# Summing a scan's pairs over the states by accumulating transfers within SBUF instead of by TensorE with the identity

## The chip, the cores and the metric

The kernel runs on one core of a Trainium2 chip. The metric is the device time of one execution in microseconds; the time before is the median of three runs. The engines are called as in the profile: PE (TensorE, with PEld for its weight loads), DVE (VectorE), ACT (ScalarE), POOL (GpSimd) and SP (SyncE, which issues most transfers).

## The reference, cut to what matters

Layer 0 is a convolution block with a Mamba scan, layer 1 attention and a mixture of eight experts. The change lies in the scan. For every batch image, in four chunks of 32 channels, it computes over a sequence of 4096 positions and N = 16 states:

```
delta = softplus(dt @ dt_proj_w.T + dt_proj_b)
dA  = exp(delta[..., None] * A)
dBu = delta[..., None] * Bm[:, :, None, :] * xin[..., None]

def step(h, inp):
    dA_t, dBu_t, C_t = inp
    h = dA_t * h + dBu_t
    y = jnp.einsum('bdn,bn->bd', h, C_t)      # the sum over the 16 states
    return (h, y)

y = y + D_skip * xin
out = y * silu(z) @ out_proj_w.T
```

The change concerns how the sum over n in y is formed. Everything is float32.

## The kernel before, in words

**Blocks, halves, states.** The sequence of one image is cut into 8 blocks of 512 positions, and there are 4 images, so 32 blocks. A block has two halves p (two channel chunks each, which fill 128 partitions), and each half has the 16 states n. A unit is one (image, block, half, state): 1024 units in all. The main loop walks through them, one unit to a slot.

**A slot.** SP fetches the B and C rows of a later unit (`rows`, three slots ahead, four buffers). ACT makes `da` two slots ahead. DVE runs three instructions on 128x512 tiles in `scan`: h = rows*du, the scan itself, and hc = rows*h, the term of this state for y. Into the same slot go one group of attention work (four score matmuls `sc`, two exponentials `pT`, and four `av` matmuls of the group before) and some stages of two lanes, X and Y. These are lists of generators for all other work: normalisations, convolution and projections of the next blocks in lane Y, the end of a block (`closed`) and the end of the network (`finished`) in lane X. Attention starts only when the first blocks of an image are closed, and a stretch of attention is left over after the last unit.

**Order.** Each engine's instructions are chained in the order in which the program writes them (`queued`), so an engine that waits for one instruction holds back all that is written after it. Waits between engines come from the tiles that instructions share, and from buffers of a pool that are taken again.

**The sum over the states.** In the first 128 slots (`ALONE`, half an image, where there is little attention yet) each term hc goes to PE one slot later and is added into one PSUM tile y by a matmul with the identity: 16 matmuls to a sum. After that POOL adds the odd state's term to the even one's (`gpsimd.tensor_add(even, even, hc)`), and PE adds the pair's sum into y two slots later: 8 matmuls to a sum. Each such matmul of float32 is two records in the trace. After the last one `scanned` lets DVE compute xin = xin*dsk + y and POOL multiply it by the gate zs; when the second half of a block is done, `closed` is put at the head of lane X.

**Buffers.** The terms hc have five buffers before. PSUM tile y has one.

A profile shows nearly all instructions under line 445, that of the recording helper, so groups are told apart by their tiles.

Of the kernel before, what the change touches and what calls it, by code (L numbers as in the profile page):

```python
# [9 lines left out]
F32 = mybir.dt.float32  # L10
# [3 lines left out]
ALU = mybir.AluOpType  # L14
# [3 lines left out]
P = 128  # L18
C = 128
EPS = 1e-5  # L20
BLK = 512
# [3 lines left out]
NST = 16  # L25
# [11 lines left out]
def conv_mamba_attn_moe_kernel(ctx: ExitStack, tc: tile.TileContext, t: dict):  # L37
    nc = tc.nc
    x, out = t["x"], t["out"]
# [19 lines left out]
    ident = const.tile([P, P], F32, name="ident")  # L59
# [379 lines left out]
    class Queue:  # L439
# [7 lines left out]
    tensor, vector, scalar, gpsimd, sync = (  # L447
        Queue(e) for e in (nc.tensor, nc.vector, nc.scalar, nc.gpsimd, nc.sync)
    )

    def mm(out, lhsT, rhs, start=True, stop=True):
        tensor.matmul(out, lhsT=lhsT, rhs=rhs, start=start, stop=stop)
# [11 lines left out]
    def flush():  # L464
        for entry in outgoing:
            entry[0] -= 1
            if entry[0] == 0:
                sync.dma_start(out=entry[1], in_=entry[2])
        outgoing[:] = [entry for entry in outgoing if entry[0]]
# [7 lines left out]
    def pool(name, bufs=1, space=None):  # L477
        return main.enter_context(
            tc.tile_pool(name=name, bufs=bufs, **({} if space is None else {"space": space}))
        )  # L480

    mix, att, side = pool("mix"), pool("att"), pool("side")
# [249 lines left out]
    def fetched(b, i, p, n):  # L732

        bcd = in_of[b, i, p][4]
        w = mix.tile([P, 2, BLK], F32, name="rows", bufs=4)
        sync.dma_start(
            out=w.rearrange("p k q -> p (k q)"),
            in_=bcd[:, n, :][None].to_broadcast([DI, 2, 2 * BLK]),
        )
        return w  # L740

    def decayed(b, i, p, n):
        da = mix.tile([P, BLK], F32, name="da", bufs=3)
        scalar.activation(da, in_of[b, i, p][2], AF.Exp, scale=amat[:, n : n + 1])
        return da

    def scan(b, i, p, n, w, da):

        du = in_of[b, i, p][3]
        h = mix.tile([P, BLK], F32, name="h", bufs=3)  # L750
        vector.tensor_mul(h, w[:, 0, :], du)
        vector.tensor_tensor_scan(
            out=h, data0=da, data1=h, initial=0.0 if i == 0 else states[b % 2][:, p, n : n + 1],
            op0=ALU.mult, op1=ALU.add,
        )
        hc = mix.tile([P, BLK], F32, name="hc", bufs=5)
        vector.tensor_mul(hc, w[:, 1, :], h)
        return h, hc

    def scanned(b, i, p, y):  # L760
        xin, zs, delta, du, bcd = in_of.pop((b, i, p))
        vector.scalar_tensor_tensor(xin, xin, dsk, y, ALU.mult, ALU.add)
        gpsimd.tensor_mul(zs, xin, zs)
        gated[b, i, p] = zs
# [185 lines left out]
    def weighted(group):  # L950
        b, q, h, pTs, first, last, prev, final = group
        if first:
            sums[0] = ps_av.tile([P, BLK], F32, name="av")
        av = sums[0]
        for k, (v, pT) in enumerate(pTs):
            for u in range(2):
                mm(
                    av[64 * u : 64 * u + 2 * DH, :], v, pT[:, u, :],
                    first and k == 0, last and k == STEP - 1,
                )  # L960
        if last:
            avs = att.tile([P, BLK], F32, name="avs", bufs=2)
            scalar.copy(avs, av)
            if prev is not None:
                gpsimd.tensor_add(avs, avs, prev)


            if not final:
                partial[b, q, h] = dram.tile([P, BLK], F32, name=f"avd{q}{h}")
                send(partial[b, q, h], avs, 3)  # L970
                return
            if h == 0:
                total[b, q] = dram.tile([2, 2, NH, DH, BLK], F32, name=f"total{q}")
            d = total[b, q]
            send(d[:, :, h].rearrange("u k r q -> (u k) r q"), avs, 3)
            if h == NH - 1:
                work_left = inverted(b, q)
                later.extend((slot + n, work_left) for n in (4, 6, 8))
# [148 lines left out]
    def advance(lane, second):  # L1127

        if inside[lane] != second:
            return False  # L1130
        while True:
            if lane not in running:

                tasks = lanes[lane] if lanes[lane] or slot < len(units) else lanes["X"]
                if not tasks or not all(k in done for k in tasks[0][2]):
                    return False
                key, stages, _ = tasks.popleft()
                running[lane] = key, stages(lane) if callable(stages) else stages
            key, stages = running[lane]
            try:  # L1140
                next(stages)
                inside[lane] = not second
                return True
            except StopIteration:
                assert not second
                done.add(key)
                del running[lane]

    def until(key):
        while key not in done:  # L1150
            flush()
            count = len(done)
            moved = [
                advance(*half) for half in (("X", True), ("Y", False), ("Y", True), ("X", False))
            ]
            assert any(moved) or len(done) > count, key
# [17 lines left out]
    for k in range(-2, len(blocks)):  # L1174
        if 0 <= k:
            b, i = blocks[k]
            Y.append((("in", b, i, 1), inputs(b, i, 1), [("scan", *blocks[k - 1], 1)] if k else []))
        if k + 2 < len(blocks):
            b, i = blocks[k + 2]
            if k + 2 == 0 or i > 0:  # L1180
                upper(k + 2)
        if 0 <= k + 1 < len(blocks):
            b, i = blocks[k + 1]
# [20 lines left out]
    ALONE = NB // 2 * 2 * NST  # L1204
    rows, decays, old, due = {}, {}, None, deque()
    even, y_of, waiting, slot = None, {}, None, 0
    while slot < len(units) or due or waiting or left or later or lanes["X"] or running:
        flush()

        for ahead in range(slot if slot == 0 else slot + 3, min(slot + 4, len(units))):  # L1210
            until(("in", *units[ahead][:3]))
            rows[ahead] = fetched(*units[ahead])
        if old:
            (b, i, p, n), h = old
            if i < NB - 1:
                scalar.copy(states[b % 2][:, p, n : n + 1], h[:, BLK - 1 : BLK])
            old = None
        for ahead in range(slot if slot == 0 else slot + 2, min(slot + 3, len(units))):
            decays[ahead] = decayed(*units[ahead])
        group = next(groups, None)  # L1220
        if slot < len(units):
            unit = units[slot]
            h, hc = scan(*unit, rows.pop(slot), decays.pop(slot))
            old = unit, h
            b, i, p, n = unit

            if slot < ALONE:
                due.append((slot + 1, unit, hc, n == 0))
            elif n % 2 == 0:
                even = hc  # L1230
            else:
                gpsimd.tensor_add(even, even, hc)
                due.append((slot + 2, unit, even, n == 1))
        advance("X", True)
        advance("Y", False)
        while due and due[0][0] <= slot:
            _, unit, term, first = due.popleft()
            b, i, p, n = unit
            if first:
                y_of[b, i, p] = ps_y.tile([P, BLK], F32, name="y")  # L1240
            mm(y_of[b, i, p], ident, term, first, n == NST - 1)
            if n == NST - 1:
                scanned(b, i, p, y_of.pop((b, i, p)))
                done.add(("scan", b, i, p))
                if p == 1:
                    lanes["X"].appendleft((("closed", b, i), closed(b, i), []))
        advance("Y", True)
        if waiting:
            weighted(waiting)
        waiting = group  # L1250
        advance("X", False)
        while later and later[0][0] <= slot:
            next(later.popleft()[1])
        slot += 1
# [6 lines left out]
    with tc.If(nc.values_load(general[0:1, 0:1]) > 0):  # L1261
# [4 lines left out]
        with tc.For_i(0, B, 1) as b:  # L1266
# [3 lines left out]
                out=t_tok.rearrange("p k c -> p (k c)"),  # L1270
                in_=tsave[bass.ds(b, 1)].rearrange("o p q -> (o p) q"),
# [96 lines left out]
```

## The time and the profile before

| | |
|---|---|
| time before | 5587.63 us, median of 3 (5581.73 to 5599.81) |
| profiled execution | span 5600.4 us, mean granted PE clock 0.944 |
| POOL adds of pairs, hc<-hc | 448, 655.8 us busy, 1465 ns mean |
| PE matmuls y<-hc,ident | 1152 records, 661.5 us busy |
| DVE scans h with a start state | 896, 1311.3 us busy, 1464 ns mean |
| DVE products hc<-rows,h | 1024, 802.2 us busy, 783 ns mean |
| DVE xin<-xin,w_dsk,y | 64, 47.6 us busy; 91.5 us idle before them |
| data moved | 1097.91 MB, mean 196 GB/s |
| hardware queue q1 | 1093.17 MB, 58.5% of 16 engines' span |

Busy time is the time in which an engine had at least one instruction of the group running. Slices cut the span into 40 equal parts of 140 us, and a digit is the busy share in tenths. The chain of work that ended last is followed back from the last instruction: shares there say which work stood on the path that set the end. A line of waits names the waiting engine and tile, what it waited for, and then the total in us, how often, and the longest. In a group's line the idle time after the second bar is that of the engine just before these instructions.

### The profile page before, as it was taken

How to read it: one execution, taken by the hardware profiler on the slowest of the kernel's cores; microseconds unless marked ns; L12 is line 12 of the kernel's file. 1: busy time of each engine (PE TensorE's matmuls, PEld its weight loads, DVE VectorE, ACT ScalarE, POOL GpSimd, SP SyncE). 2: the span in 40 equal slices, each digit the busy share in tenths (PEclk: the TensorE clock that was granted, in tenths of full speed). 3: DMA queues.
4: the chain of work that ended last, by engine and by line, in shares of the span. 5: the costliest groups of instructions: out<-in, count | busy, mean ns of one | idle time of the engine just before them, and what ended most of it. 6: DMA issues, size and time to landing. Idle time of an engine off the chain costs nothing.

```text
span 5600.4 us, 60586 instructions
## 1 busy us (share of the span) xinstructions
PE 4916.5 (88%) x17866; PEld 2040.8 (36%) x17866; DVE 4174.5 (75%) x6275; ACT 3892.2 (69%) x5957; POOL 2161.8 (39%) x1885
## 2 busy tenths in 40 slices
PE   4666798988999988999998899898999989899997
PEld 2222333333333333333333333333333333344343
DVE  4888877887888888887887888887888888741221
ACT  3455587787777777787777777687777777666553
POOL 2333444454444444445443444444444443320000
PEclk7777799999999999999999999999999999999998
DMA  3455566666666666667665556666765666654432
GB/s 95 169 171 176 194 210 210 205 228 211 230 208 203 210 208 216 205 225 229 224 211 192 192 200 213 219 221 209 232 223 202 206 205 209 210 183 154 147 121 67
DMA packets 427635, 1097.91 MB, mean 196 GB/s; under 512 B 48401, under 2 KB 131746, under 8 KB 427298
## 3 DMA queue, kind: packets, MB, share of 16 engines
q1 hardware_dynamic: 426130, 1093.17, 58.5%
q8 instruction: 144, 2.36, 0.2%
q14 instruction: 193, 1.58, 0.1%
q10 hardware_dynamic: 1168, 0.80, 0.1%
HBM read 941.95 MB, written 135.00 MB: 192 GB/s over the span
## 4 chain that ended last, share of the span: by engine, by line
PE 45%; DVE 21%; ACT 15%; issue 7%; POOL 6%; DMA 5%; SPq 1%; DVEq 0%; ACTq 0%; POOLq 0%
PE av L445 17%; DVE h L445 11%; PE sc L445 10%; PE ps_X L445 8%; PE ps_Y L445 5%; ACT pT L445 5%; PE y L445 4%; ACT L445 3%; ACT xt L445 3%; DVE hc L445 2%; DVE cm L445 2%; POOL rsY L445 1%; POOL rsX L445 1%; DMA ks<-kd 1%; ACT da L445 1%
## 5 line engine op out<-in xcount | busy, mean ns | idle before, releaser
L445 ACT ACTIVATE pT<-sc 128x1024 f32<-128x1024 f32 x2048 | 1983.7, 1022 | 1017.6 <-PE sc L445 1015.2
L445 PE MATMUL av<-pT,v 128*64 128x512 f32 x8192 | 2004.9, 610 | 3.5 <-ACT avs L445 3.3
L445 DVE TENSOR_TENSOR_SCAN h<-da,state,h 128x512 f32<-128x512 f32 x896 | 1311.3, 1464 | 118.6 <-ACT da L445 26.8
L445 PE MATMUL sc<-qs,ks 128*128 128x512 f32 x4096 | 1308.8, 440 | 96.9 <-DMA ks<-kd 51.9
L445 POOL TENSOR_TENSOR hc<-hc 128x512 f32<-128x512 f32 x448 | 655.8, 1465 | 1718.7 <-DVE hc L445 1513.3
L445 PEld LDWEIGHTS sc<-qs,ks 128*128 128x128 f32 x4096 | 717.7, 193 | 773.7 <-ACT pT L445 283.0
L445 PEld LDWEIGHTS av<-pT,v 128*64 128x64 f32 x8192 | 501.6, 137 | 1193.3 <-issue 1105.8
L445 DVE TENSOR_TENSOR h<-rows,du 128x512 f32<-128x512 f32 x1024 | 830.6, 811 | 88.0 <-ACT state L445 38.1
L445 DVE TENSOR_TENSOR hc<-rows,h 128x512 f32<-128x512 f32 x1024 | 802.2, 783 | 78.3 <-DVE h L445 2.3
L445 ACT ACTIVATE da<-delta,amat 128x512 f32<-128x512 f32 x1024 | 749.4, 732 | 9.4 <-DVE h L445 5.2
L445 PE MATMUL y<-hc,ident 128*128 128x512 f32 x1152 | 661.5, 662 | 62.4 <-DVE hc L445 51.3
L445 ACT ACT_TABLE_LOAD x319 | 409.3, 1283 | 22.9 <-PE ps_Y L445 17.8
L445 ACT COPY state<-h 128x1 f32<-128x1 f32 x896 | 175.7, 196 | 194.8 <-DVE h L445 194.3
L445 PEld LDWEIGHTS y<-hc,ident 128*128 128x128 f32 x1152 | 219.6, 209 | 213.8 <-DVE hc L445 101.4
L445 POOL TENSOR_SCALAR rsY<-mvY 128x4 f32<-128x4 f32 x99 | 57.5, 581 | 527.3 <-DVE mvY L445 523.2
L445 POOL TENSOR_TENSOR avs<-avs,prev 128x512 f32<-128x512 f32 x64 | 89.3, 1396 | 438.1 <-ACT avs L445 319.7
L445 PE MATMUL ps_X<-share,w_ew 128*128 128x512 f32 x448 | 223.9, 622 | 20.5 <-DVE share L445 20.2
L445 ACT ACTIVATE xt<-ps_Y,shiftY,rsY 128x128 f32<-128x128 f32 x380 | 143.2, 462 | 129.9 <-POOL shiftY L445 122.4
L445 POOL TENSOR_SCALAR du<-e 128x512 f32<-128x512 f32 x64 | 145.9, 2280 | 217.2 <-ACT e L445 217.2
L445 DVE TENSOR_TENSOR share<-share,xf 128x1024 f32<-128x1024 f32 x128 | 182.8, 1428 | 51.1 <-DMA share<-sharesY 31.0
L445 DVE RECIPROCAL den<-den 128x32 f32<-128x32 f32 x16 | 5.5, 346 | 265.6 <-DMA den<-total 265.6
L445 DVE TENSOR_TENSOR_SCAN h<-da,h 128x512 f32<-128x512 f32 x128 | 182.9, 1429 | 17.3 <-ACT da L445 4.4
(234 smaller groups left out, 4729.6 us busy)
## 6 DMA issues: line engine op xcount, KB each, us to landing
rows<-bcd SPq DMA_DIRECT2D x1024, 512.0 KB
ks<-kd SPq DMA_DIRECT2D x256, 512.0 KB
qs<-qd SPq DMA_DIRECT2D x129, 512.0 KB
v<-vd SPq DMA_DIRECT2D x256, 256.0 KB
share<-sharesX SPq DMA_DIRECT2D x112, 512.0 KB
pairs<-xn SPq DMA_DIRECT2D x128, 128.5 KB
qd<-hi SPq DMA_DIRECT2D x32, 512.0 KB
qd<-lo SPq DMA_DIRECT2D x32, 512.0 KB
```

The source lines that it names most:

```text
L445: return lambda *args, **kw: queued(op(*args, **kw))
```

## The change

Outside the first 128 slots PE no longer adds the pairs' sums. The pair of states 0 and 1 is summed by POOL into a tile of its own, ysum, in SBUF (two buffers). Each of the seven later pairs is summed by POOL as before, and then a transfer issued from POOL adds it into ysum, reading and writing SBUF (`accum_op=ALU.add`). PE's 448 identity matmuls of these slots fall away; those of the first 128 slots stay. `scanned` still comes two slots after the last state and reads ysum. The terms hc have four buffers in place of five. What it is for: TensorE is the engine with the largest busy share, and this sum needs none of its multiplying.

```diff
-        hc = mix.tile([P, BLK], F32, name="hc", bufs=5)
+        if n == 0 and slot >= ALONE:
+            hc = mix.tile([P, BLK], F32, name="ysum", bufs=2)
+        else:
+            hc = mix.tile([P, BLK], F32, name="hc", bufs=4)
         vector.tensor_mul(hc, w[:, 1, :], h)
         return h, hc
...
             if slot < ALONE:
                 due.append((slot + 1, unit, hc, n == 0))
             elif n % 2 == 0:
                 even = hc
             else:
                 gpsimd.tensor_add(even, even, hc)
-                due.append((slot + 2, unit, even, n == 1))
+                if n == 1:
+                    y_of[b, i, p] = even
+                else:
+                    gpsimd.dma_start(out=y_of[b, i, p], in_=even, accum_op=ALU.add)
+                if n == NST - 1:
+                    due.append((slot + 2, unit, None, False))
...
             if first:
                 y_of[b, i, p] = ps_y.tile([P, BLK], F32, name="y")
-            mm(y_of[b, i, p], ident, term, first, n == NST - 1)
+            if term is not None:
+                mm(y_of[b, i, p], ident, term, first, n == NST - 1)
             if n == NST - 1:
                 scanned(b, i, p, y_of.pop((b, i, p)))
```

## The prediction

> **What bounds the kernel now.** I read four views in this order: the page's busy shares and slices (is any engine full, and where), busy time by stretch, the chain that ended last (what a unit of saved work is worth), and the waits of VectorE (who holds whom). First the page, sections 1 and 2.
>
> ```profile
> PE 4916.5 (88%) x17866; PEld 2040.8 (36%) x17866; DVE 4174.5 (75%) x6275; ACT 3892.2 (69%) x5957; POOL 2161.8 (39%) x1885
> ...
> PE   4666798988999988999998899898999989899997
> ...
> DVE  4888877887888888887887888887888888741221
> ...
> DMA  3455566666666666667665556666765666654432
> ```
>
> Between the fifth and the thirty-fifth slice PE is near full, DVE stands at 8 and DMA at 6. After that there are no more scan slots, only attention. The change touches slots 128 to 1023; the following stretch runs from slot 156 to the last scan.
>
> ```profile
> 700.00:4966.00 4266.00, 3885.40 (x14502) 1612.82 (x14502) 3519.72 (x5126) 3210.24 (x4922) 1873.88 (x1582) 0.97 0.63 213
> ```
>
> The columns are PE, PEld, DVE, ACT, POOL, then granted clock, DMA share and GB/s. The stretch holds 868 scans (counted in the timeline of DVE), so a slot takes 4266/868 = 4.91 us: PE is busy for 4.48 of it (91%), DVE 4.05, ACT 3.70, POOL 2.16. PE is the fullest engine, but three of them lie within 0.8 us, and none is at 100%. So a saving on PE can't come through in full: DVE is the next wall at 4.05.
>
> The chain by line (section 4) says what is on the path:
>
> ```profile
> PE 45%; DVE 21%; ACT 15%; issue 7%; POOL 6%; DMA 5%; SPq 1%; DVEq 0%; ACTq 0%; POOLq 0%
> PE av L445 17%; DVE h L445 11%; PE sc L445 10%; PE ps_X L445 8%; PE ps_Y L445 5%; ACT pT L445 5%; PE y L445 4%; ACT L445 3%; ACT xt L445 3%; DVE hc L445 2%; DVE cm L445 2%; POOL rsY L445 1%; POOL rsX L445 1%; DMA ks<-kd 1%; ACT da L445 1%
> ```
>
> The matmuls to remove (y) hold 4% of it, 224 us. DMA holds 5% already, so landings count in this kernel. The waits of DVE from 1000 to 5000 us, longest first:
>
> ```profile
> DVE res L445 <- PE ps_X L445: 69.0, 34, 7.4
> DVE hi L445 <- PE ps_X L445: 68.7, 15, 8.8
> DVE xin L445 <- PE y L445: 65.4, 34, 9.3
> DVE prX L445 <- PE ps_X L445: 50.1, 16, 9.0
> DVE gn L445 <- DMA gn<-in_x: 30.5, 8, 14.1
> DVE aT L445 <- DMA inv<-inverse: 29.0, 12, 6.1
> ```
>
> DVE's waits for PE add up to about 350 us over all rows of that answer; those for DMA to about 100.
>
> [...] The trace of before has no transfer of that kind: all its data went by hardware queues issued from SyncE and ScalarE. [...] The nearest thing in the trace, the pairs<-xn copies within SBUF (four of 128.5 KB), shows 2.37 us at best in the chain of waits and 9.24 us at worst. [...] in one stretch around 4004 us with POOL running without a gap, scans took 2.11 us, where 1.23 to 1.28 us is usual. The POOL adds stay, so this cost stays.
>
> **The change, part by part.**
>
> *Removed from PE.* Outside the first 128 slots there were 448 pair sums of two matmul records each. From 1000 to 5000 us:
>
> ```profile
> L445 PE MATMUL y<-hc,ident 128*128 128x512 f32 x804 | 433.6, 622 | 7.5 <-POOL hc L445 7.5
> ```
>
> 804 records are 402 sums, 1.08 us each, 0.54 us a slot. PE falls to 4.48 - 0.54 = 3.94 us a slot, just under DVE. How much of 0.54 arrives? The chain gives 224 us over the span, 0.25 a slot, as what was surely on the path. DVE's waits for PE, 350 us in 4000, give 0.43 a slot if all vanished. I take 0.30 a slot, 868 x 0.30 = 260 us. The weight loads of y (PEld) lie beside other matmuls and bring nothing more.
>
> *Added: the transfers.* There are 56 sums over 16 states left (64 less 8 in the first 128 slots), with 8 pairs each; the first pair stays where POOL added it, and seven are accumulated, so 392 transfers of 256 KB. The hardware queue moved 1093.17 MB in 58.5% of 16 engines' span: 1093.17/(0.585 x 5600.4) = 334 GB/s while busy. A copy of 256 KB is 0.785 us on all engines[...]. [...] what is in flight beside an accumulation comes later. Some 36 DMA pieces stand on the chain between 700 and 5000 us, mostly 4 to 9 us long; each meets about one accumulation (one per pair of slots, 9.8 us)[...]: 50 us.
>
> *Added: their latency.* In the order of the built program three things wait for it. POOL's next accumulation waits for the one before (336 times). On DVE the multiply writing hc waits for the transfer that reads that buffer, since hc has four buffers now (335 times, three slots after the pair's second term). And xin in scanned, also on DVE, waits for the last transfer (56 times, two slots after the last term), where it waited for PE before. Behind POOL's wait are queued rs and shift of the two lanes, for which ScalarE's xt waits; behind DVE's waits stands the whole scan. The latency L is not in the trace. Lower bound 3.2 us (2.37 us of pairs[...]), upper bound 9.24 us (pairs in a busy stretch). Slot lengths in the stretch: a tenth are at 2.7 us, the quartiles 3.4, 4.5 and 5.8. I stepped through these 868 lengths, each 0.38 shorter but not under 2.72 (which takes the 260 us off), with 1.46 us for POOL's add (its row)[...] and the three waits. The waits then add 10 us for L = 4, 93 for 6, 195 for 7, 349 for 8, 576 for 9. I take L = 6, the middle of the bounds: the transfers have a queue of their own but share engines that are 63% busy. 93 us.
>
> *Added: POOL's time.* [...] Hidden: POOL waited 1386 us for DVE's hc in 4000 us, with nothing else to do.
>
> *Moved.* y lies in SBUF now, so xin reads two SBUF operands (0.75 us as before), and the first hc of a sum comes from its own two buffers, with 16 slots until reuse: nothing. PE's queue loses waits for hc (7.5 us): nothing.
>
> Sum: -260 + 93 + 50 = -117 us, so 5587.6 - 117 = about 5470.
>
> **The rivals.** *(R1) The transfers are hidden wholly.* L at 4 or less, no collisions; PE gives 0.40 a slot: -347 + 10, 5250 us. For: DMA is idle 37% of the time, hc has slack of three slots. Against: gn, inv and pairs already wait for landings. *(R2) The chain of accumulations becomes the bound.* L of 9 to 10 us: the pair can't be shorter than the latency plus its issue, about 10 us against a median of 9.5 for two slots now. Waits of 576 to 866 us, with -260 and +50 as above: 5950 to 6240 us; the sum turns positive already at L of about 7.1. For: 9.24 us on pairs; against: that row queued behind half a dozen transfers of its own ring. *(R3) PE was not the pace-setter.* DVE and the lanes take back the gain, and collisions cost the rest: 5580 to 5600 us. For: PE idles 9% in the stretch; against: 750 us of ScalarE's waits there are pT waiting for PE's sc.
>
> **How the numbers follow.** Forecast 0.45, R1 0.14, R2 with all L above 7.2 0.34, R3 0.07. Faster 0.59, same 0.07, slower 0.34. The time is that of the forecast, 5470. The range runs from R1 (5240) to L of about 8.6 (waits of 475 us, 5850), and leaves out the worse part of R2, some 0.16, and a little under R1.
>
> **What would show it.** Right: y gone from the chain; a slot of 4.6 to 4.8 us; PE down by about 480 us in busy time; a new DVE wait of hc and xin for ysum's transfers below 120 us together; DMA share at 75 to 80%. Wrong: hc or xin waiting for a transfer at the top of DVE's list, or POOL's accumulations waiting for each other for many hundred us (R2); PE idle grown by as much as y gave, with DVE's waits on others instead (R3); DMA share grown by 30 points or more[...].

## The result, and the profile after

The changed kernel takes 5726.09 us (median of four, 5721.36 to 5730.98), the kernel before 5589.66 us beside it: ratio 1.0243, 95% interval 1.0223 to 1.0264, so 136 us slower. The forecast was 5470.

First the page of the changed kernel: the busy shares, and the slices of PE, DVE, the granted clock and DMA.

```profile
PE 4690.0 (82%) x16970; PEld 1936.1 (34%) x16970; DVE 4202.8 (73%) x6275; ACT 3892.2 (68%) x5957; POOL 2480.9 (43%) x2277
...
PE   4676788887888887888888888787888888889997
...
DVE  4888877777888888877887888787887888750221
...
PEclk8777798898999998998999999898998999999998
DMA  3455777777777777777776677777876777764432
```

PE lost 226 us of busy time, although the removed matmuls held 485 (661.5 less the 176.6 of the first 128 slots that stay). The nines of PE turned into eights, and so did some of the clock's: from 700 us on, the granted clock is 0.92 (to 4966 us), where it was 0.97. The columns of the stretch are the same as in the prediction's; the kernel is slower now, so the same stretch holds fewer of its instructions.

```profile
700.00:4966.00 4266.00, 3564.21 (x13229) 1471.71 (x13228) 3446.38 (x5008) 3124.84 (x4813) 2128.81 (x1919) 0.92 0.74 229
```

The last product of a scan starts at 5084.5 us in place of 4966.2 (the tile hc), and what follows is as long as before, 635 us. Slot 128, the first changed one, starts its scan at 575.7 us in place of 576.9. So all the loss lies in the 896 slots that were changed.

The chain that ended last, by engine and by line:

```profile
PE 30%; DVE 19%; POOL 14%; ACT 12%; DMA 12%; issue 10%; SPq 1%; DVEq 0%; POOLq 0%; ACTq 0%
PE av L445 11%; DVE h L445 10%; PE sc L445 7%; PE ps_X L445 6%; DMA ysum<-hc 6%; PE ps_Y L445 5%; ACT pT L445 4%; ACT L445 2%; POOL hc L445 2%; POOL rsY L445 2%; ACT xt L445 2%; POOL rsX L445 2%; POOL du L445 2%; DVE hc L445 2%; DMA ks<-kd 1%
```

PE's share fell from 45% to 30%, and POOL (6% to 14%) and DMA (5% to 12%) took it over. y has left the list, and the transfer stands there with 6%. Tile ysum shows the issue and, last, the time from issue to landing:

```profile
L445 POOL DMA_DIRECT2D ysum<-hc x392: 867/885/1102, 592.2 to 5092.2; - x196
...
DMA to landing us min/median/max: 3.3/5.6/10.5
```

The median landing, 5.6 us, is close to the 6 us that the prediction took, so the surprise isn't in the latency by itself. An issue held POOL for 0.885 us (median).

### The profile page after: what moved, and what is told of

It is laid out like the page before. It is cut to its first block, busy times and chain, and to the rows that moved or that the text cites. A ratio compares the mean times of both kernels' runs of the same rounds, so it can differ in the third digit from the quotient of the medians.

```text
span 5719.6 us, 59540 instructions
## 1 busy us (share of the span) xinstructions
PE 4690.0 (82%) x16970; PEld 1936.1 (34%) x16970; DVE 4202.8 (73%) x6275; ACT 3892.2 (68%) x5957; POOL 2480.9 (43%) x2277
## 3 DMA queue, kind: packets, MB, share of 16 engines
q0 software_dynamic: 56448, 102.79, 10.2%
## 4 chain that ended last, share of the span: by engine, by line
PE 30%; DVE 19%; POOL 14%; ACT 12%; DMA 12%; issue 10%; SPq 1%; DVEq 0%; POOLq 0%; ACTq 0%
PE av L445 11%; DVE h L445 10%; PE sc L445 7%; PE ps_X L445 6%; DMA ysum<-hc 6%; PE ps_Y L445 5%; ACT pT L445 4%; ACT L445 2%; POOL hc L445 2%; POOL rsY L445 2%; ACT xt L445 2%; POOL rsX L445 2%; POOL du L445 2%; DVE hc L445 2%; DMA ks<-kd 1%
## 5 line engine op out<-in xcount | busy, mean ns | idle before, releaser
L445 PE MATMUL av<-pT,v 128*64 128x512 f32 x8192 | 2094.3, 634 | 8.4 <-ACT avs L445 8.1
L445 PE MATMUL sc<-qs,ks 128*128 128x512 f32 x4096 | 1346.0, 450 | 147.2 <-DMA ks<-kd 75.0
L445 POOL TENSOR_TENSOR hc<-hc 128x512 f32<-128x512 f32 x392 | 583.6, 1489 | 1299.6 <-DVE hc L445 1280.6
L445 PEld LDWEIGHTS sc<-qs,ks 128*128 128x128 f32 x4096 | 736.7, 199 | 858.8 <-ACT pT L445 380.7
L445 PEld LDWEIGHTS av<-pT,v 128*64 128x64 f32 x8192 | 518.4, 142 | 1066.7 <-issue 1017.9
L445 DVE TENSOR_TENSOR hc<-rows,h 128x512 f32<-128x512 f32 x968 | 764.7, 790 | 72.9 <-DVE h L445 3.2
L445 POOL DMA_DIRECT2D ysum<-hc x392 | 351.6, 897 | 290.0 <-DMA ysum<-hc 171.7
L445 PE MATMUL ps_X<-ident,xt 128*128 128x128 f32 x372 | 109.4, 365 | 227.4 <-ACT xt L445 218.1
L445 PE MATMUL y<-hc,ident 128*128 128x512 f32 x256 | 176.6, 794 | 52.0 <-DVE hc L445 51.8
```

What stands on the lines that cost most here:

```text
L445: return lambda *args, **kw: queued(op(*args, **kw))
```

## The experiments

Each kernel was timed beside the kernel before on one chip. Since the kernel before read 5589 to 5595 us from one group to the next, differences below are to it within the group. Three theories stood at the start. **C**: without the y matmuls PE pauses long enough to lose its clock, and the relief is eaten. **Q**: POOL's queue. **D**: the load on the DMA engines and late landings.

**The relief alone** (ratio 0.9857, 0.9841 to 0.9874; -80 us).

```diff
-                    gpsimd.dma_start(out=y_of[b, i, p], in_=even, accum_op=ALU.add)
+                    pass
```

> The changed kernel without its transfers: each sum over the states keeps only the pair of states 0 and 1, the other seven pairs are left out. TensorE, VectorE and POOL adds are as in the changed kernel. Theory Q (POOL's queue: the issue, the wait for the transfer before and the wait for its own add hold back rs and shift of the lanes) and theory D (later landings of all transfers): the relief of PE comes through, 5300 to 5400 us, granted clock in the stretch from 700 us on at 0.95 or more. Theory C (without the y matmuls PE pauses long enough for its clock to be cut, 0.97 to 0.92, which eats the relief by itself): 5520 to 5600 us at a clock of about 0.92.

Measured: 5514.27 us. Neither theory has it. Theory C's range begins 6 us above it, and the clock, 0.95 in the stretch, is the one that Q and D expected. The removal of 448 sums is worth 80 us and no more, so the transfers cost 136 + 80 = 216 us on top of it. The stretch, the busy shares and the chain of this run:

```profile
700.00:4966.00 4266.00, 3678.18 (x13956) 1517.65 (x13954) 3571.80 (x5149) 3258.93 (x4981) 1906.60 (x1597) 0.95 0.65 215
...
PE 4614.9 (84%) x16970; PEld 1905.8 (35%) x16970; DVE 4218.7 (77%) x6275; ACT 3889.0 (71%) x5957; POOL 2182.7 (40%) x1885
...
PE 34%; DVE 27%; ACT 16%; DMA 7%; POOL 7%; issue 7%; SPq 1%; DVEq 0%; ACTq 0%; POOLq 0%
```

Two things took the rest. Matmuls overlap on PE, so the 661.5 us of y can't simply be taken off PE's 4916.5. Counted from the trace's records without y's matmuls, PE is busy for 4376.2 us before and for 4456.9 here. So y filled 540.2 us alone before and fills 158.0 here: 382 us of PE's time were freed. Of these, 81 went back because the other matmuls got slower, and 214 because PE's pauses grew, from 684.0 to 897.5 us in all; the traced run is 88 us shorter.

The slowing fits the clock. The trace grants PE either the full clock or half of it; PE worked at half clock for 435.3 us before and for 587.5 here. An estimate of what that costs is half of the difference, 76 us. The pauses are waits for other engines and for landings: DVE rose from 21% of the chain to 27%. DVE's own waits for PE, 1000 to 5000 us, add up to 357.5 us before and 280.5 here, so 77 us of them went.

The fewer hc buffers of the change are in this run too, and cost nothing that shows: the only waits of the product hc are 1.8 us for DVE's own h from 700 to 4900 us, and in the changed kernel it waited 1.4 us for a transfer.

**PE kept busy.** The same matmul on constants, with nothing to wait for and no reader, where each pair's sum stood.

```diff
-                if n == NST - 1:
-                    due.append((slot + 2, unit, None, False))
+                due.append((slot + 2, unit, None, False))
...
+            else:
+                mm(ps_y.tile([P, BLK], F32, name="y"), ident, ew[:, 0:4, :])
```

> The changed kernel, with a matmul on constants (identity and expert weights, result unused) on PE where each y matmul of a pair stood, so PE has the work of the kernel before and no wait for hc. Theory C: the clock returns to 0.95 or more and the time is at or below that of the changed kernel, 5640 to 5730 us. Theories Q and D: the work comes on top, 5800 to 5950 us.

Measured: 5768.65 us (1.0311, 1.0294 to 1.0328), 38 us above the changed kernel for 489 us of work on PE. Its groups on PE, and the one to compare from the changed kernel below:

```profile
L445 PE MATMUL av<-pT,v 128*64 128x512 f32 x8192 | 2005.4, 611 | 3.5 <-ACT avs L445 3.3
...
L445 PE MATMUL y<-w_ew,ident 128*128 128x512 f32 x896 | 488.9, 629 | 0.1
```

```profile
L445 PE MATMUL av<-pT,v 128*64 128x512 f32 x8192 | 2094.3, 634 | 8.4 <-ACT avs L445 8.1
```

Work that nothing waits for took the av matmuls from 634 back to 611 ns. PE's other work, counted as above, is busy for 4532.3 us in the changed kernel and for 4402.3 here, 130 less, and PE's time at half clock fell from 759.6 to 503.2 us; half of that difference is 128. So the clock follows PE's load. The constants and y together fill 543.4 us alone here, where y filled 157.7: about a third of these 386 us came back by the clock. None of the theories has the time: it is 39 us above C's range, and 31 below that of Q and D, which took work on PE at its full length.

The changed kernel's trace shows when. Every stretch at one clock from 700 to 5000 us is 3.41 us or a multiple of it. In the 3.41 us before each of the 111 drops there, PE was busy for up to 62%, a quarter in the median, and in only 16 for less than 1%. Before each return it was busy for at least 83%. Four stretches of 3.4 us, columns as before; the clock is the third number from the end:

```profile
3253.00:3256.40 3.40, 1.20 (x3) 0.29 (x2) 3.16 (x7) 2.93 (x6) 1.49 (x2) 0.98 0.94 287
3256.40:3259.80 3.40, 0.66 (x2) 0.60 (x3) 3.02 (x14) 0.55 (x1) 0.00 (x0) 0.50 1.01 308
3259.80:3263.20 3.40, 3.40 (x7) 1.04 (x6) 2.39 (x3) 2.02 (x3) 1.39 (x2) 0.52 0.90 307
3263.20:3266.60 3.40, 3.40 (x16) 1.63 (x18) 2.10 (x3) 2.86 (x4) 1.70 (x2) 1.00 0.76 169
```

The clock fell at 3256.25 us, 2 us after PE had stopped, in a wait of 4.93 us for a landing of keys. The timeline shows what follows, four score matmuls at the lower clock and, once it had returned, four at the full one:

```profile
3259.14 2.04 PE L445 MATMUL sc<-qs,ks 128*128 128x512 f32 x4 [4.93 <-DMA ks<-kd]
...
3264.34 1.17 PE L445 MATMUL sc<-qs,ks 128*128 128x512 f32 x4
```

**Is DVE the next wall?** For odd states after the first 128 slots the product rows*du is left out, once on the relief alone and once on the kernel before.

```diff
-        vector.tensor_mul(h, w[:, 0, :], du)
+        skip_it = slot >= ALONE and n % 2 == 1
+        if not skip_it:
+            vector.tensor_mul(h, w[:, 0, :], du)
...
-            out=h, data0=da, data1=h,
+            out=h, data0=da, data1=w[:, 0, :] if skip_it else h,
```

> The relief alone, and for odd states outside the first 128 slots the product rows*du is left out (the scan reads rows directly), 448 DVE instructions of about 0.7 us less. Its fall against 5514 us is compared with that of the next run against the kernel before. Theory W (after the relief DVE is the wall): the fall here is larger, 200 to 300 us. Theory C (the clock takes the relief back, whatever DVE does): the falls are alike, within 40 us.

> The kernel before with the same product left out for odd states. Theory W: PE holds it, so it falls by 50 to 130 us only. Theory C: by as much as the run with the relief.

Measured: 5409.61 us (0.9684) on the relief, 99 us below the relief alone; 5533.59 us (0.9903) on the kernel before, 56 us below that. DVE lost 377 us of busy time in the first and 372 in the second, so its work is worth nearly twice as much once y is gone. That is W's direction, but far below its 200 to 300 us, and the falls differ by 44 us, which the noise doesn't tell from the 40 that C allowed: DVE is a larger part of the limit than before, not the wall by itself. How the missing 180 of the 260 us divide between clock and DVE isn't settled, since no run holds the clock.

**Small transfers.** As many issues with as many rows, 16 columns each.

```diff
-                    gpsimd.dma_start(out=y_of[b, i, p], in_=even, accum_op=ALU.add)
+                    gpsimd.dma_start(out=y_of[b, i, p][:, 0:16], in_=even[:, 0:16], accum_op=ALU.add)
```

> The changed kernel with the same 392 accumulating transfers, of 16 columns in place of 512 (the other columns of seven pairs are left out of the sums). POOL issues as many with as many rows; the DMA engines have next to nothing to move. The relief alone gave 5514 us, the changed kernel 5726: 212 us are the transfers. Theory Q (POOL's issue, its wait for its own add and the order of its queue): 5640 to 5700 us. Theory D (the load on the DMA engines and landings that come later): 5520 to 5570 us. The wait for the transfer before and that of xin shrink with the latency, which takes about 32 us (two-sums run) in either case.

Measured: 5640.11 us (1.0092, 1.0074 to 1.0109), +48 us to the kernel before and so 128 us above the relief. It is Q's range, at its lower edge. With hardly any bytes, six tenths of the transfers' cost are there. What POOL waited for at the issue, 700 to 4900 us, and what ScalarE then waited for:

```profile
POOL ysum L445 <- POOL hc L445: 101.4, 331, 1.0
ACT xt L445 <- POOL shiftY L445: 98.5, 64, 4.2
ACT xt L445 <- POOL shiftX L445: 93.3, 40, 7.5
...
POOL ysum L445 <- DMA ysum<-hc: 49.5, 26, 5.5
```

The first line is the issue waiting for POOL's own add, 0.3 us each time. The two lines of xt are the lanes' normalisations behind it in POOL's queue: 192 us together. In the relief alone they read:

```profile
ACT xt L445 <- POOL shiftY L445: 65.1, 53, 2.5
ACT xt L445 <- POOL shiftX L445: 49.2, 37, 4.1
```

PE waits for xt in turn, in the same stretch for 153 us in the relief alone and for 220 here, and pauses.

**POOL's time alone.** A memset without waits where the issue stood, from the second image on.

```diff
-                    gpsimd.dma_start(out=y_of[b, i, p], in_=even, accum_op=ALU.add)
+                    if b:
+                        gpsimd.memset(taps[:, 0:8, :], 0.0)
```

> The relief alone, and in place of each transfer from the second image on (336 of 392) a memset of 128x1024 into the tile of the taps on POOL, about as long as the issue of a transfer, with no wait and no reader; seven pairs of each sum are left out. If POOL's time itself is what the issues cost: 5600 to 5640 us, near the 5640 of the small transfers. If it is the waits of the issue (for POOL's own add, 101 us, and for the transfer before, 50 us): 5520 to 5560 us.

Measured: 5567.14 us (0.9941, 0.992 to 0.9962), 52 us above the relief. A memset took 952 ns, so for 392 issues of 897 ns about 57 us are POOL's time itself, on an engine that is busy for 40% of the span. That is a little above the 5520 to 5560 that was expected if the waits count, and well below the other range. The two xt lines read 90.4 and 64.1 here, so they rise with the time. The other 70 of the 128 go with the issue's waits and the latency of even a small transfer (4.2 us to landing), which weren't taken apart.

**The load without POOL.** Two plain copies of 256 KB for each pair, in the hardware queue, from the second image on.

```diff
-                    gpsimd.dma_start(out=y_of[b, i, p], in_=even, accum_op=ALU.add)
+                    for k in (0, 4) if b else ():
+                        send(taps[:, k : k + 4, :].rearrange("p k c -> p (k c)"), even)
```

> The relief alone, and for each pair from the second image on two plain copies of 256 KB within SBUF, issued by SyncE one slot later into the tile of the taps, which nothing reads; seven pairs of each sum are left out. POOL issues nothing. [...] Theory D: 5650 to 5750 us. Theory Q: 5520 to 5560 us. The copies stand in the hardware queue ahead of rows, so a time above 5750 would be that order and not the load.

Measured: 5562.02 us (0.9952, 0.9941 to 0.9963), 50 us above the relief for 48 of 56 sums, so some 58 for all. That is 2 us above Q's range and 88 below D's: the load is real but small. The DMA share from 700 to 4900 us is 0.75 here and 0.74 in the changed kernel, so the engines are as full. Still it's a figure from a neighbour: copies in another queue aren't accumulations.

**Two sums.** Every other accumulation goes elsewhere, so a transfer waits for the one two pairs back.

```diff
-                    gpsimd.dma_start(out=y_of[b, i, p], in_=even, accum_op=ALU.add)
+                    total_of = y_of[b, i, p] if b == 0 or n % 4 == 3 else taps[:, 0:4, :].rearrange("p k c -> p (k c)")
+                    gpsimd.dma_start(out=total_of, in_=even, accum_op=ALU.add)
```

> The changed kernel, but from the second image on every other accumulation goes into a second tile (that of the convolution's taps, no longer read then), so that a transfer waits only for the one two pairs earlier; the second partial sum is left out of the result. Theory Q: POOL's 247 us of waiting for the transfer before go nearly to nothing and the time falls by 60 to 120 us, to 5600 to 5670. Theories D and C: within 30 us of the changed kernel.

Measured: 5694.45 us (1.0186, 1.0169 to 1.0203), 37 us below the changed kernel, each taken to the kernel before beside it. That is the chain between transfers, as far as this run loosens it: under the 60 to 120 us of Q, and a little over the 30 of D and C. The three parts, 128, 58 and 37, come to 223 against 216. But they aren't separate: the small transfers still wait for one another (49.5 us above), so a piece of the chain is in the 128 as well. That the sum is near doesn't show that the division is right.

**Issue at the slot's end.**

```diff
-                    gpsimd.dma_start(out=y_of[b, i, p], in_=even, accum_op=ALU.add)
+                    late.append((y_of[b, i, p], even))
...
         advance("X", False)
+        for total_of, pair in late:
+            gpsimd.dma_start(out=total_of, in_=pair, accum_op=ALU.add)
+        late.clear()
```

> The changed kernel with each accumulating transfer issued at the end of its slot, after the stages of both lanes, so that rs and shift of that slot stand ahead of it in POOL's queue; same transfers, same waits for one another. POOL alone cost 126 us (small transfers against the relief alone). Theory Q1 (what hurts is that lane work stands behind the issue in POOL's queue): 5620 to 5680 us, and xt waiting for shift falls from 206 us towards the 114 of the relief alone. Theory Q2 (POOL's added time hurts wherever it stands): 5700 to 5740 us.

Measured: 5758.59 us (1.0305, 1.0287 to 1.0322), 33 us above the changed kernel. Q1's mechanism shows and its time doesn't: xt's waits for shift, 700 to 4900 us, fell from 206 to 148 us. But the transfers land later in their slots, and the two lines below were 154.3 and 61.5 us in the changed kernel. So what POOL's order alone costs isn't shown by this run.

```profile
POOL ysum L445 <- DMA ysum<-hc: 284.4, 96, 8.3
...
DVE xin L445 <- DMA ysum<-hc: 187.1, 44, 10.3
```

**Transfers beside the y matmuls.** Both at once, xin reading y in PSUM.

```diff
                 gpsimd.tensor_add(even, even, hc)
+                if n == 1:
+                    ysum = even
+                else:
+                    gpsimd.dma_start(out=ysum, in_=even, accum_op=ALU.add)
```

> PE adds the pairs into y as in the kernel before and xin reads that; beside it POOL issues the 392 accumulating transfers into ysum, which nothing reads. hc has four buffers. Theories Q and D: the transfers' full cost on top of the kernel before with no relief, 5850 to 5950 us. Theory C: the clock stays at 0.96 to 0.97 in the stretch and the transfers cost little, 5620 to 5720 us, below the changed kernel.

Measured: 5977.58 us (1.0691), which says nothing of the theories: PE's first matmul of a sum came after the first transfer into the tile it reads, so it also read a sum with the second pair in it, and it held PE's queue (700 to 4900 us):

```profile
PE y L445 <- DMA ysum<-hc: 205.4, 48, 11.4
```

So once more, with that matmul one slot earlier (slot + 1 where n is 1):

> As the run with transfers beside the y matmuls, but the first pair's matmul comes one slot earlier, ahead of the first transfer into the same tile: there PE waited 194 us for that transfer and held its whole queue. Expected if the transfers cost on top of the kernel before what they cost on top of the relief (212 us): 5800 us. Theory C (a busier PE keeps its clock and so hides part): 5700 to 5760 us. If the two costs add up more than singly: above 5850 us.

Measured: 5768.6 us (1.0314, 1.0295 to 1.0334), +177 us. The transfers cost less beside the matmuls than on top of the relief (216), in between the two expectations.

**Other ways to make the sum.** POOL adds the pairs' sums into ysum:

```diff
-                    gpsimd.dma_start(out=y_of[b, i, p], in_=even, accum_op=ALU.add)
+                    gpsimd.tensor_add(y_of[b, i, p], y_of[b, i, p], even)
```

> A version that computes the whole sum and issues no transfer: POOL adds each later pair's sum into ysum itself, 392 more adds of about 1.47 us, 576 us on POOL, which the changed kernel's issues and waits took to about 600. Theory D: 5530 to 5600 us, faster than or even with the kernel before. Theory Q: about the changed kernel's, 5680 to 5760 us, since POOL's queue is as full[...].

Measured: 5800.28 us (1.0381, 1.036 to 1.0402), above both ranges and worse than the transfers: DVE's busy time rose from the changed kernel's 4202.8 to 4506.4 us, and the mean product hc from 790 to 876 ns. That fits 392 more POOL adds: in the changed kernel's trace, from 700 to 4966 us, hc took 860 ns on average where POOL was busy all through it (134 products) and 692 ns where POOL was idle (469). PE adds every term, in all slots:

```diff
-    ALONE = NB // 2 * 2 * NST
+    ALONE = len(units)
```

> The opposite change, a version that computes the whole: in all slots PE adds each single term into y, POOL adds no pairs. PE gets 448 more sums of about 1.08 us, 484 us; POOL loses 656 us of adds. If a sum on PE costs only what the relief gave back per sum (80 us for 448) and POOL's time is dear (126 us for 392 issues of about 1.2 us): 5400 to 5550 us. If PE, at 91% in the stretch, has no more room: 5750 us or more.

Measured: 5667.39 us (1.0141, 1.0124 to 1.0158). That is in neither of the expected ranges. PE is 64% of that chain, and its clock in the stretch is 0.99: here it is nearest to being the wall. The 78 us are net of what POOL and DVE gained (656.8 and 217.5 us of busy time), so what the sums alone cost isn't known. Last, transfers add the odd term to the even one, PE sums the pairs a slot later, hc has six buffers:

```diff
-        hc = mix.tile([P, BLK], F32, name="hc", bufs=5)
+        hc = mix.tile([P, BLK], F32, name="hc", bufs=6)
...
-                gpsimd.tensor_add(even, even, hc)
-                due.append((slot + 2, unit, even, n == 1))
+                gpsimd.dma_start(out=even, in_=hc, accum_op=ALU.add)
+                due.append((slot + 3, unit, even, n == 1))
```

> A version that computes the whole and uses the transfers elsewhere: the accumulating transfer adds the odd state's term to the even one's in place of POOL's add, and PE sums the pairs into y as before, one slot later; hc has six buffers. POOL's 448 adds of 1465 ns become 448 issues of about 0.9 us with no wait for one another[...]. If POOL's time and its hold on DVE are what counts: 5480 to 5570 us, faster than both. If the load and the landings count for more: 5600 to 5680 us.

Measured: 5630.97 us (1.0063, 1.0044 to 1.0082). The busy shares and the chain:

```profile
PE 4922.8 (87%) x17866; PEld 2039.2 (36%) x17866; DVE 3992.2 (71%) x6275; ACT 3894.5 (69%) x5957; POOL 1877.5 (33%) x1885
...
PE 45%; DVE 20%; ACT 14%; DMA 9%; issue 6%; POOL 4%; SPq 1%; DVEq 0%; ACTq 0%; POOLq 0%
```

DVE lost 182 us and POOL 284, with PE as before at 45% of the chain, and DMA went from 5% to 9%: what was freed gave less than the transfers took. Which part of their cost it was, load, landings or issue, this run doesn't tell. No version tried that computes the whole beats the kernel before.

## Why the prediction was wrong, by its own steps

*Removed from PE.* The step that failed. The relief was put at 260 us and measured 80. The 485 us of busy time were sized right, but alone they filled only 382 us of PE, since the rest ran beside other matmuls. The 260 came from two readings: the chain (224, taken as surely on the path) and DVE's waits for PE (350, if all vanished). Both hold the rest of the kernel fixed. In the run 77 us of those waits vanished. With y gone, PE pauses 214 us more, its clock falls and its other matmuls take 81 us more, and DVE, 0.43 us a slot behind, takes a larger part of the path.

*POOL's time*, put at nothing because POOL waited 1386 us for hc. It cost about 57 us, and with the issue's waits and what is left of a small transfer's latency 128. That idle time was real but didn't stand where the issue came: rs and shift follow behind in an ordered queue, and xt's waits for them rose with each of these costs. This is the second term that was mis-sized, from 0 upward.

*Latency of the transfers.* L was 5.6 us for the assumed 6, with 3.3 us for the fastest landing, and an issue took 0.9 us. Loosening the chain between transfers was worth 37 us; the prediction had 93 us for the three waits, the author's estimate with a length of the issue that no trace had shown. The waits themselves are longer, 171.7 us at the issue, 75.5 at xin and 1.4 at hc over the span, but before the change xin waited 91.2 us for PE. Right in kind; whether 93 was the right size no run shows.

*Load.* 50 us predicted, the author's estimate: no trace of before showed what an accumulation takes of the DMA engines. About 58 by the neighbour run, which isn't an accumulation, so the agreement may be chance. In the changed kernel the queue q0 moved 102.79 MB in 10.2% of 16 engines' span, 102.79/(0.102 x 5719.6) = 176 GB/s, 1.9 times slower than the 334 of the hardware queue. What makes it slower no run shows. PE's waits for landings of keys (sc for ks) rose from 51.9 to 75.0 us over the span. The DMA share of 0.74 is just below the foreseen 0.75.

Had the relief been 80 as measured, the prediction's own costs (143) would have given +63, slower, with the right sign. The other 73 us are the costs, 216 in place of 143. Of its signs of being right, y left the chain and hc and xin waited 77 us together, under 120; but a slot took 5.04 us and not 4.6 to 4.8, and PE's busy time fell by 226 us and not by 480.

*The rivals.* R3 (PE was not the pace-setter) was nearest to the mechanism: PE's idle time grew by 346 us, its own sign. It was given 0.07, for the reason that ScalarE waited for PE. R2 had the side right for a reason that didn't hold: the accumulations did not become the bound.

## What to carry to other kernels

A share of the chain is what a piece of work took, not what its removal gives; where PE's clock follows its load, take PE's work as partly free in both directions, and look for the second engine before pricing a relief. Count what a group of matmuls fills alone: its busy time also holds what runs beside others. An engine's idle total doesn't hide new work on it if its queue is ordered and short work of other chains stands right behind: price it by who is next in that queue. Here only the waits show that, and moving the issue behind that work made the kernel slower. To split the cost of a transfer, run it once with next to no bytes, once as a plain load on another queue, and once with nothing but the issuing engine's time; these parts overlap, so their sum proves nothing.

## What the runs showed of the hardware that wasn't expected

- A matmul with no purpose speeds up the others: 489 us of constants' work on PE lengthened the run by 38 us, and took PE's other work from 4532 to 4402 us.
- PE's clock fell by half though PE was still at work part of the time: in the 3.41 us before the 111 drops from 700 to 5000 us of the changed kernel it was busy for up to 62%, a quarter in the median.
- An accumulating transfer of 256 KB within SBUF took 3.3 to 10.5 us to land, median 5.6; of 8 KB still 2.0 to 9.0, median 4.2. The bytes are the smaller part of these medians.
- Its issue held POOL for 0.885 us (median) with 128 rows, whether these had 16 columns or 512, and about 0.3 us more waiting for POOL's own add before it.
